# Two additions moved from VectorE into TensorE's accumulations, with ScalarE copying the sums out of PSUM, in a Mamba block with two gated feed-forwards

## The chip, the cores and the metric

The kernel runs on one core of a Trainium2 chip. The time is the device time of one execution in microseconds (us). The core's engines are TensorE (PE in the profile; PEld is its loading of weights), VectorE (DVE), ScalarE (ACT), GpSimd (POOL) and SyncE (SP), which here only issues transfers (DMA). Each engine works through its own list of instructions in order and waits for the others by semaphores; a transfer is issued by an engine's queue and carried out by the core's 16 DMA engines.

## The reference, cut to what matters

The input x has 4 sequences of 1024 tokens and 256 features, all in float32.

```python
u  = rmsnorm(layernorm(x)) * norm1_w
z, xb, B, C, dt = split(u @ in_proj.T)             # per token
dt = softplus(dt @ dt_proj.T + bias)               # 256 channels
h_t = exp(dt_t * A) * h_{t-1} + (dt_t * xb_t) * B_t   # 32 states a channel
y  = sum_states(h * C) + D_param * xb              # "D x"
hr = layernorm(x) + (y * silu(z)) @ out_proj.T
hr = hr + (silu(xn @ gate.T) * (xn @ up.T)) @ down.T      # xn = rmsnorm(hr)
x1 = x + hr
out = x1 + fwht(silu(n @ W1.T) * (n @ W3.T)) @ W2.T       # n = layernorm(x1)
```

The change touches two of these sums: `D_param * xb` in y, and the residual rows `hr` (with x already added to them in the kernel) behind the down projection.

## The kernel before, in words

Work goes by chunks of 512 tokens: 8 chunks, numbered 0 to 7, two to a sequence. Even chunks are first halves of a sequence and their scans start from zero; odd chunks are second halves, whose scans start from states that POOL kept (L783). Each chunk has 16 steps, n = 0 to 15, and a step is a sixteenth of the 8192 channel-state rows: four blocks of 128 partitions by 512 tokens. For a step q

- SP issues a transfer of dt, spread over the partitions, into `da` (L704 through `dma_da`, 1 MB, four buffers), and two of dt times xb into `ub` (512 KB each, six buffers);
- ACT takes the exponential of `da` in place (L741, four of 128x512), running one step ahead of the scans;
- DVE multiplies `ub` by B, which lies in PSUM as `pb`, into `bx` (L765, two of 128x1024), and scans `da` in place (L774, four of 128x512);
- POOL multiplies the states by C, with `cr` from a transfer (L784, one of 128x2048);
- PE sums over the states into `py` in PSUM (L795, four products into four 32-partition strips, which run side by side). Steps 0 to 7 go to one `py`, steps 8 to 15 to the next; `py` has one buffer.

A `da` buffer is free again when PE has summed its step, so the transfer for step q + 4 is issued after the sums of step q.

`y_dx` (L810, DVE) then makes yt = x * D + py in one operation, and `y_z` (L815, POOL) multiplies it by silu(z). Both happen twice a chunk, once behind n = 7 and once behind n = 15.

`pb` is written once for eight steps by `copy_b` (L754): at n = 0 of a chunk by ACT, at n = 8 by DVE.

All else of the block (norms, projections, two gated feed-forwards) is laid between the steps. The order is written by hand: a tick is half a step, `at(tick, lane, function)` puts a function on a tick, and the loop at the end of `tile_block` runs each tick's lanes in the order PE, ACT, `times_b`, ACTb, two exponentials (of the next step), a scan, DVE, a scan, POOL0, `times_c`, POOL, `sum_states`, PEend, ACTend, SP, `dma_ub`, `dma_da`, `dma_cr`, SPend. There are 32 ticks to a chunk. E is the first tick behind a chunk's own steps, which is the first tick of the next chunk, and what `post` does for a chunk it does at E + something, beside the next chunk's steps:

- E+2 (ACTend): ACT's copies of a later chunk's transposed input and of the rest of the second feed-forward before it. E+3: `hr` = layernorm(x) (ACT, L200); out projection on PE from yt and `wo` (`add_rows`, L306); its sums are copied by ACT (`evict`, L321) and added by POOL (`add_pool`, L325) for chunks 0 to 6.
- E+4 to E+7: on PE the down projection of the second feed-forward of the chunk before (`w2h`, L306).
- E+5 to E+9: row sums by ACT (`row_stats`, L170 and L173), the root on POOL (L195, L196), scaled rows on ACT (L200), transposes on PE (L213); x is added to `hr` by POOL (L659).
- E+10 to E+16: first gated feed-forward: projections on PE (L226, `gated`), silu (L263) and copies (L270) on ACT, products on POOL (L274).
- E+18 to E+21: down projection by `add_rows` with `wd`, one 128-token group a tick (L306). Its sums of two groups at a time are added to `hr` by DVE in `add` (L316), at E+20 and E+22.
- E+20 to E+25: row sums of `hr` by ACT behind that (ACTend of E+20 and E+22), the root on POOL, scaled rows on ACT, transposes on PE.
- E+26 to E+39: second gated feed-forward (L226 from `xt`) and its down projection; the store at E+43.

For chunk 7 all of this comes behind the last scan, as a tail. There the sums of the out projection and of the last down projection are added by DVE (`add`).

Of the kernel before, what the change touches and what calls it, by code (L numbers as in the profile page):

```python
# [9 lines left out]
F32 = mybir.dt.float32  # L10
AF = mybir.ActivationFunctionType
ALU = mybir.AluOpType
# [3 lines left out]
P = 128  # L16
# [4 lines left out]
TT = T // P  # L21
# [6 lines left out]
def tile_block(ctx: ExitStack, tc: tile.TileContext, a, out):  # L28
# [20 lines left out]
    nc = tc.nc  # L49

    wp = ctx.enter_context(tc.tile_pool(name="w", bufs=1))
    p1 = ctx.enter_context(tc.tile_pool(name="p1", bufs=1))
# [4 lines left out]
    sm = ctx.enter_context(tc.tile_pool(name="sm", bufs=4))  # L57
# [23 lines left out]
    us = [{"b": b, "c": c} for b in range(BATCH) for c in range(SEQ // T)]  # L81
    load_x(us[0])
    n1 = load("n1", [P, 2], a["n1"])
    ident = load("ident", [P, P], a["ident"])
# [8 lines left out]
    dpar = load("dpar", [P, 2], a["dpar"])  # L93
    rsel = load("rsel", [P, 8, 32], a["rsel"])

    mhalf = wp.tile([P, TT], F32, tag="mhalf", name="mhalf")
    nc.vector.memset(mhalf, -0.5)
    w2h = wp.tile([P, 8, DM], F32, tag="w2h", name="w2h")
# [83 lines left out]
    def row_stats_first(u, src):  # L182

        u["mv"] = sm.tile([P, 2, TT], F32, tag="mv", name="mv")
        st = sm.tile([P, TT, 6], F32, tag="st", name="st")
        ag = sm.tile([P, TT, 2], F32, tag="ag", name="ag")
        for t in range(TT):
            nc.vector.bn_stats(st[:, t, :], src[:, t, :])
        for t in range(TT):
            nc.vector.bn_aggr(ag[:, t, :], st[:, t, :])  # L190
        nc.vector.tensor_copy(u["mv"][:, 1, :], ag[:, :, 1])
        nc.vector.tensor_scalar(u["mv"][:, 0, :], ag[:, :, 0], -1.0 / 16, None, ALU.mult)
# [45 lines left out]
    def at(tick, lane, fn, *args):  # L238
        todo[tick][lane].append(partial(fn, *args))
# [53 lines left out]
        for i in range(1, len(chunks)):  # L293
            at(tick + 3, "POOL", product, i)

    def add_rows(tick, u, lhs, rhs, per_tick, lane="PE", on_pool=False):

        po = {}

        def pe(t):  # L300
            if t % 2 == 0:
                po[t // 2] = dense_psum().rearrange("p (t d) -> p t d", t=2)
            left, right = lhs(), rhs()
            n = len(left)
            for k in range(n):
                nc.tensor.matmul(  # L306
                    po[t // 2][:, t % 2, :],
                    lhsT=left[k][:, t * P : (t + 1) * P],
                    rhs=right[k],
                    start=(k == 0),  # L310
                    stop=(k == n - 1),
                )

        def add(i):
            hr = u["hr"][:, 2 * i : 2 * i + 2, :]
            nc.vector.tensor_tensor(hr, hr, po[i], ALU.add)  # L316

        def evict(i):
            ev = p3.tile([P, T], F32, tag="up", name="ev")
            po[i] = ev.rearrange("p (t d) -> p t d", t=2), po[i]  # L320
            nc.scalar.copy(*po[i])  # L321

        def add_pool(i):
            hr = u["hr"][:, 2 * i : 2 * i + 2, :]
            nc.gpsimd.tensor_tensor(hr, hr, po[i][0], ALU.add)  # L325

        for t in range(TT):
            at(tick + t // per_tick, lane, pe, t)
            if t % 2:
                after = tick + t // per_tick + 1  # L330
                if on_pool:
                    at(after, "ACTend", evict, t // 2)
                    at(after + 1, "POOL", add_pool, t // 2)
                else:
                    at(after, "DVE", add, t // 2)
# [268 lines left out]
    def post(u, E, other):  # L604
# [31 lines left out]
        def store():  # L636
# [11 lines left out]
            lambda: [W["wo"][:, k, :] for k in range(2)],  # L648
            4,
            "PEend",  # L650
            on_pool=u is not us[-1],
        )
        at(E + 5, "ACTend", lambda: row_stats(u, u["hr"], (0, 1), False))
        at(E + 6, "ACTend", lambda: row_stats(u, u["hr"], (2, 3), False))
# [8 lines left out]
        for i in range(2):  # L663
# [5 lines left out]
            lambda: [u["m"][:n, c, :] for c, n in enumerate(sizes)],  # L669
            lambda: [W["wd"][:n, c, :] for c, n in enumerate(sizes)],  # L670
            1,
        )
        at(E + 20, "ACTend", lambda: row_stats(u, u["hr"], (0, 1)))
        at(E + 22, "ACTend", lambda: row_stats(u, u["hr"], (2, 3)))
# [6 lines left out]
        for i in range(3):  # L681
# [4 lines left out]
            lambda: [u["g"][:, c, :] for c in range(8)],  # L686
            lambda: [w2h[:, c, :] for c in range(8)],
            1,
            on_pool=u is not us[-1],
        )  # L690
        at(E + 43, "SPend", store)

# [95 lines left out]
    def sum_states(q):  # L788
        s = qs[q]
        u = s["u"]  # L790
        first, last = s["n"] % 8 == 0, s["n"] % 8 == 7
        if first:
            u["py"] = ps_y.tile([P, T], F32, tag="y", name="py")
        for b in range(4):
            nc.tensor.matmul(  # L795
                u["py"][32 * b : 32 * b + 32, :],
                lhsT=rsel[:, 2 * s["j"] + s["g"], :],
                rhs=s["da"][:, b, :],
                start=first,
                stop=last,  # L800
            )
        if last:
            at(2 * q + 4, "DVE", y_dx, u, s["h"])
            at(2 * q + 5, "POOL0", y_z, u, s["h"])


    def y_dx(u, h):
        if h == 0:
            u["yt"] = p3.tile([P, 2, T], F32, tag="T", name="yt")
        nc.vector.scalar_tensor_tensor(  # L810
            u["yt"][:, h, :], u["xr"][:, h, :], dpar[:, h : h + 1], u["py"], ALU.mult, ALU.add
        )

    def y_z(u, h):
        nc.gpsimd.tensor_tensor(u["yt"][:, h, :], u["yt"][:, h, :], u["zs"][:, h, :], ALU.mult)  # L815


    for k, u in enumerate(us):
# [8 lines left out]
    at(-20, "PE", wake_pe)  # L827
    at(-18, "ACTend", load_first)
    at(-17, "ACTend", weights_ready)
    at(-2, "DVE", times_b, 0, 0)  # L830
    at(-2, "SP", dma_da, 1)
    at(-1, "SPend", dma_cr, 0)
# [129 lines left out]
```

## Time and profile before

| what | us |
|---|---|
| median of three runs (lowest, highest) | 1163.14 (1161.78, 1168.64) |
| the profiled execution | 1173.07 |
| its span, from the first instruction to the last | 1171.2 |
| scans, from the first of chunk 0 to the end of the last of chunk 7 | 22.07 to 1053.61 |
| chunks 1 to 7 begin with their first scan at | 160.10, 286.51, 416.64, 544.81, 672.90, 801.46, 926.98 |
| busy: PE, DVE, ACT, POOL | 959.6, 962.9, 782.2, 887.1 |
| `y_dx` L810, 16 of 128x512 | 11.7 busy, 733 ns each |
| `add` L316, 20 of 128x512 (14 of them before 1050 us, six in the tail) | 13.4 busy, 669 ns each |
| `copy_b` L754 on ACT, 7; on DVE, 8 | 592 ns, 674 ns each |
| ACT's copies out of PSUM of 128x512, L270 | 579 ns each |
| granted clock of TensorE, mean | 0.899 |

How to read it: "busy" is the time in which an engine had an instruction under way; a row `out<-in` of the profile names the tile written and those read; in a list of waits the numbers are the idle time in total, how often, and the longest; a row of the timeline has its start, its length, the engine, the line, the operation and how many instructions were merged, and in brackets how long the engine had been idle before it and what ended that. PE's records of one float32 product are two. Matmul records overlap, since PE is pipelined, so the length of a merged row divided by its count says more than the mean length of one record.

### The profile page before, as it was taken

The page shows a single profiled execution, that of the slowest core. Times are in us where ns is not written, and L with a number is a line of the kernel's source. Part 1 is how long each engine was busy: PE and PEld are TensorE (multiplying, and loading weights), DVE is VectorE, ACT ScalarE, POOL GpSimd, SP SyncE. Part 2 cuts the span into 40 slices and gives each one's busy share as a digit, 9 for nine tenths or more (in the row PEclk, how much of TensorE's full clock was granted, in tenths as well). Part 3 has the DMA queues.
Part 4 walks back from the last instruction along what each step waited for, and adds up shares of the span by engine and source line. Part 5 has one row for each costly group of instructions (what it writes and reads, how often), then busy time and mean ns, then how long its engine had stood idle before and what let it go on. Part 6 is the DMA issues. An engine that isn't in the chain of part 4 may idle for free.

```text
span 1171.2 us, 11883 instructions
## 1 busy us (share of the span) xinstructions
PE 959.6 (82%) x3374; PEld 456.5 (39%) x3374; DVE 962.9 (82%) x840; ACT 782.2 (67%) x1411; POOL 887.1 (76%) x515
## 2 busy tenths in 40 slices
PE   8464236969998799969996999979997987799978
PEld 3121012423634255423633364424543362336535
DVE  4897799999998989999999899999999899990000
ACT  3835556868768786779677786878685967563331
POOL 6675758878978888878977998789977898674312
PEclk9777558979899799979998899979997999789989
DMA  7989999898799889997799889988799789730000
GB/s 252 352 300 351 353 327 308 311 325 296 250 340 320 300 298 320 319 327 281 270 348 325 281 300 334 319 325 297 270 310 360 281 291 343 262 111 1 18 0 18
DMA packets 89441, 321.89 MB, mean 275 GB/s; under 512 B 9312, under 2 KB 20000, under 8 KB 73120
## 3 DMA queue, kind: packets, MB, share of 16 engines
q1 hardware_dynamic: 87520, 318.38, 77.1%
q10 hardware_dynamic: 1856, 2.75, 0.7%
q8 instruction: 27, 0.44, 0.1%
q14 instruction: 38, 0.31, 0.1%
HBM read 302.22 MB, written 18.87 MB: 274 GB/s over the span
## 4 chain that ended last, share of the span: by engine, by line
PE 25%; DMA 7%; DVE 6%; POOL 6%; issue 5%; ACT 4%; DVEq 0%; POOLq 0%; ACTq 0%; SPq 0%
PE dense L226 14%; PE dense L306 8%; DMA da<-dtd 5%; POOL da L784 4%; DVE da L774 3%; DVE bx L765 3%; PE py L795 3%; DMA ub<-ud 2%; ACT da L741 1%; POOL m L274 1%; POOL g L274 1%; DVE hr L316 0%; ACT up L270 0%; ACT L741 0%; ACT junk L173 0%
## 5 line engine op out<-in xcount | busy, mean ns | idle before, releaser
L784 POOL TENSOR_TENSOR da<-da,cr 128x2048 f32<-128x2048 f32 x128 | 580.0, 4531 | 86.8 <-DVE da L774 22.5
L741 ACT ACTIVATE da<-da,nega 128x512 f32<-128x512 f32 x508 | 334.4, 713 | 170.8 <-DMA da<-dtd 159.3
L774 DVE TENSOR_TENSOR_SCAN da<-da,carry,bx 128x512 f32<-128x512 f32 x256 | 315.7, 1268 | 20.0 <-DVE bx L765 7.6
L774 DVE TENSOR_TENSOR_SCAN da<-da,bx 128x512 f32<-128x512 f32 x256 | 300.2, 1209 | 37.0 <-ACT da L741 21.3
L765 DVE TENSOR_TENSOR bx<-ub,pb 128x1024 f32<-128x1024 f32 x254 | 312.2, 1229 | 20.3 <-ACT pb L754 9.3
L795 PE MATMUL py<-da,rsel 128*32 128x512 f32 x1024 | 162.5, 712 | 159.4 <-POOL da L784 159.4
L226 PE MATMUL dense<-xt,w 128*128 128x512 f32 x512 | 238.4, 621 | 1.4 <-ACT si L263 1.4
L226 PEld LDWEIGHTS dense<-xt,w 128*128 128x128 f32 x512 | 99.4, 199 | 145.9 <-issue 123.4
L795 PEld LDWEIGHTS py<-da,rsel 128*32 128x32 f32 x1024 | 21.4, 115 | 243.0 <-POOL da L784 201.2
L306 PE MATMUL dense<-w2h,g 128*128 128x256 f32 x512 | 113.4, 380 | 0.0
L274 POOL TENSOR_TENSOR g<-si,up 128x512 f32<-128x512 f32 x64 | 80.5, 1272 | 32.3 <-ACT up L270 32.2
L306 PEld LDWEIGHTS dense<-w2h,g 128*128 128x128 f32 x512 | 96.8, 190 | 18.4 <-ACT ev L321 2.5
L306 PE MATMUL dense<-wd,m 128*128 128x256 f32 (+1 forms) x384 | 98.2, 400 | 0.9 <-POOL m L274 0.9
L316 DVE TENSOR_TENSOR hr<-hr,dense 128x512 f32<-128x512 f32 x20 | 13.4, 669 | 99.9 <-PE dense L306 99.9
L226 PE MATMUL dense<-ut,win 128*128 128x512 f32 x192 | 94.7, 625 | 0.2 <-ACT ut L220 0.2
L270 ACT COPY up<-dense 128x512 f32<-128x512 f32 x112 | 63.4, 579 | 46.8 <-PE dense L226 46.4
L274 POOL TENSOR_TENSOR m<-si,up 128x512 f32<-128x512 f32 (+1 forms) x48 | 60.2, 1270 | 43.5 <-ACT up L270 43.5
L226 PE MATMUL dense<-ht,wg 128*128 128x512 f32 x192 | 87.7, 600 | 3.4 <-ACT ht L220 3.4
L306 PEld LDWEIGHTS dense<-wd,m 128*128 128x128 f32 (+1 forms) x384 | 68.6, 192 | 37.6 <-issue 20.6
L263 ACT ACTIVATE si<-dense 128x512 f32<-128x512 f32 x112 | 60.7, 596 | 28.4 <-PE dense L226 25.5
L226 PE MATMUL dense<-ht,wu 128*128 128x512 f32 x160 | 72.8, 600 | 4.8 <-ACT si L263 4.8
L741 ACT ACT_TABLE_LOAD x44 | 56.5, 1283 | 4.8 <-DMA da<-dtd 4.0
(95 smaller groups left out, 798.6 us busy)
## 6 DMA issues: line engine op xcount, KB each, us to landing
da<-dtd SPq DMA_DIRECT2D x127, 1024.0 KB
ub<-ud SPq DMA_DIRECT2D x254, 512.0 KB
cr<-cd SPq DMA_DIRECT2D x64, 256.0 KB
x<-in_x SPq DMA_DIRECT2D x8, 512.0 KB
dtd<-dt SPq DMA_DIRECT2D x16, 256.0 KB
ud<-du SPq DMA_DIRECT2D x16, 256.0 KB
cd<-cc SPq DMA_DIRECT2D x16, 256.0 KB
out<-hr SPq DMA_DIRECT2D x8, 512.0 KB
```

The lines of the kernel that those rows point to most:

```text
L226: nc.tensor.matmul(dst[:n], lhsT=w[:, k, col : col + n], rhs=src[:, k, :], start=(k == 0), stop=(k == 1),)
L263: nc.scalar.activation(g[i]["si"][:n], g[i]["pg"][:n], AF.Silu)
L270: nc.scalar.copy(g[i]["up"][:n], g[i]["pu"][:n])
L274: nc.gpsimd.tensor_tensor(u[dst][:n, c, :], g[i]["si"][:n], g[i]["up"][:n], ALU.mult)
L306: nc.tensor.matmul(po[t // 2][:, t % 2, :], lhsT=left[k][:, t * P : (t + 1) * P], rhs=right[k], start=(k == 0), stop=(k == n - 1),)
L316: nc.vector.tensor_tensor(hr, hr, po[i], ALU.add)
L741: nc.scalar.activation(da, da if q else s["u"]["pdt", b], AF.Exp, scale=an[:, s["h"], s["j"], b, s["g"] : s["g"] + 1],)
L765: nc.vector.tensor_tensor(s["bx"], s["ub", b0 // 2], u["pb"].unsqueeze(1).broadcast_to([P, 2, T]), ALU.mult)
L774: nc.vector.tensor_tensor_scan(da, da, s["bx"][:, b % 2, :], start, ALU.mult, ALU.add)
L784: nc.gpsimd.tensor_tensor(s["da"], s["da"], s["cr"].unsqueeze(1).broadcast_to([P, 4, T]), ALU.mult)
L795: nc.tensor.matmul(u["py"][32 * b : 32 * b + 32, :], lhsT=rsel[:, 2 * s["j"] + s["g"], :], rhs=s["da"][:, b, :], start=first, stop=last,)
```

## The change

D x becomes part of PE's accumulation in `py`. At the start, ACT makes two diagonal matrices of D (`dd`, one for each half of the channels) from the identity. Where a `py` begins (n = 0 and n = 8), PE first multiplies `dd` by `xr`, the rows of x, into it (start of the accumulation), and the sums over the states add to that. `y_dx` is gone. In its place ACT copies `py` to `yt` at the end of the same tick (lane ACTend), and `y_z` follows on POOL as before. For the last `py` of all there is no copy: DVE multiplies `py` by silu(z) at once.

In `add_rows` with `wd`, each 128-token group begins with a product of the identity with the residual rows `hr`, and the six products of the down projection add to it. `add` on DVE becomes a copy by ACT, `replace`, from PSUM into `hr`, at the same ticks in lane ACTend, ahead of the row sums that read it. This holds for all eight chunks. The other two uses of `add_rows` stay as they were.

Two small tiles of the very first row statistics move to a pool with one buffer; no instruction changes by that.

```diff
+    dd = wp.tile([P, 2, P], F32, tag="dd", name="dd")
+
+    def diagonal(h):
+        nc.scalar.activation(dd[:, h, :], ident, AF.Identity, scale=dpar[:, h : h + 1])
...
-        st = sm.tile([P, TT, 6], F32, tag="st", name="st")
-        ag = sm.tile([P, TT, 2], F32, tag="ag", name="ag")
+        st = p1.tile([P, TT, 6], F32, tag="st", name="st")
+        ag = p1.tile([P, TT, 2], F32, tag="ag", name="ag")
...
+            dst = po[t // 2][:, t % 2, :]
+            if way == "pe":
+                rows = u["hr"][:, t, :]
+                nc.tensor.matmul(dst, lhsT=ident, rhs=rows, start=True, stop=False)
             for k in range(n):
                 nc.tensor.matmul(
-                    po[t // 2][:, t % 2, :],
+                    dst,
                     lhsT=left[k][:, t * P : (t + 1) * P],
                     rhs=right[k],
-                    start=(k == 0),
+                    start=(k == 0 and way != "pe"),
                     stop=(k == n - 1),
                 )
...
+        def replace(i):
+            nc.scalar.copy(u["hr"][:, 2 * i : 2 * i + 2, :], po[i])
...
-                if on_pool:
+                if way == "pe":
+                    at(after, "ACTend", replace, t // 2)
+                elif way == "pool":
                     at(after, "ACTend", evict, t // 2)
                     at(after + 1, "POOL", add_pool, t // 2)
                 else:
...
         if first:
             u["py"] = ps_y.tile([P, T], F32, tag="y", name="py")
+            x = u["xr"][:, s["h"], :]
+            nc.tensor.matmul(u["py"], lhsT=dd[:, s["h"], :], rhs=x, start=True, stop=False)
         for b in range(4):
...
-                start=first,
+                start=False,
                 stop=last,
             )
         if last:
-            at(2 * q + 4, "DVE", y_dx, u, s["h"])
-            at(2 * q + 5, "POOL0", y_z, u, s["h"])
-
-
-    def y_dx(u, h):
+            if q == NQ - 1:
+                at(2 * q + 4, "DVE", y_z_last, u)
+            else:
+                at(2 * q + 4, "ACTend", y, u, s["h"])
+                at(2 * q + 5, "POOL0", y_z, u, s["h"])
+
+
+    def y(u, h):
         if h == 0:
             u["yt"] = p3.tile([P, 2, T], F32, tag="T", name="yt")
-        nc.vector.scalar_tensor_tensor(
-            u["yt"][:, h, :], u["xr"][:, h, :], dpar[:, h : h + 1], u["py"], ALU.mult, ALU.add
-        )
+        nc.scalar.copy(u["yt"][:, h, :], u["py"])
...
+    def y_z_last(u):
+        nc.vector.tensor_tensor(u["yt"][:, 1, :], u["py"], u["zs"][:, 1, :], ALU.mult)
...
+    for h in range(2):
+        at(1, "ACTend", diagonal, h)
```

More of the change, by code (lines that the diff above doesn't have):

```diff
@@ L294, in gated, with add_rows @@
             at(tick + 3, "POOL", product, i)
-    def add_rows(tick, u, lhs, rhs, per_tick, lane="PE", on_pool=False):
+    def add_rows(tick, u, lhs, rhs, per_tick, lane="PE", way=None):
         po = {}
@@ L650, in post @@
             "PEend",
-            on_pool=u is not us[-1],
+            way="pool" if u is not us[-1] else None,
         )
@@ L671, in post @@
             1,
+            way="pe",
         )
@@ L688, in post @@
             1,
-            on_pool=u is not us[-1],
+            way="pool" if u is not us[-1] else None,
         )
```

## The prediction

> **What bounds the kernel now.** I read the page's busy shares first, then the busy time by stage, the waits of VectorE (DVE), and the timeline where a chunk begins and where its second half runs. Chunks, steps (n = 0 to 15), ticks and E are those of the section on the kernel.
>
> ```profile
> PE 959.6 (82%) x3374; PEld 456.5 (39%) x3374; DVE 962.9 (82%) x840; ACT 782.2 (67%) x1411; POOL 887.1 (76%) x515
> ```
> Two engines share the first place. Chunks 4 and 5 by themselves:
>
> ```profile
> core 0: us, PE busy (x) PEld busy (x) DVE busy (x) ACT busy (x) POOL busy (x), PEclk, DMA share, GB/s
> ...
> 545.00:671.00 126.00, 112.20 (x403) 54.21 (x402) 115.75 (x100) 94.55 (x175) 107.80 (x67) 0.92 0.85 305
> 671.00:801.00 130.00, 118.40 (x432) 56.00 (x430) 121.95 (x102) 101.89 (x185) 110.38 (x56) 0.95 0.89 313
> ```
> DVE works 92 to 94% of such a stretch, PE 89 to 91%, DMA 85 to 89%. Three resources stand within 6% of each other, so DVE's share alone doesn't settle what an edit on it is worth. Its waits do more:
>
> ```profile
> DVE hr L316 <- PE dense L306: 99.9, 6, 43.9
> DVE da L774 <- ACT da L741: 21.5, 18, 4.2
> DVE yt L810 <- PE py L795: 12.5, 7, 8.9
> ...
> DVE bx L765 <- ACT pb L754: 9.3, 3, 4.1
> ```
> The 99.9 us are the tail behind the scans, where DVE has nothing else to do. The last line is the one that matters: at the start of chunks 3, 5 and 7 DVE stands still (3.16, 4.09 and 2.04 us in the timeline) for ScalarE's (ACT's) copy L754. How ACT comes to be late there, in chunk 4:
>
> ```profile
> 616.64 0.51 SPq L704 DMA_DIRECT2D da<-dtd  x1
> ...
> 621.90 1.06 PE L795 MATMUL py<-da,rsel 128*32 128x512 f32 x8 [0.18 <-POOL da L784]
> ...
> 622.90 6.03 PE L306 MATMUL dense<-wd,m 128*128 128x256 f32 x24
> ...
> 629.83 1.33 ACT L741 ACTIVATE da<-da,nega 128x512 f32<-128x512 f32 x2 [4.82 <-POOL carry L783]
> ...
> 640.31 0.19 POOL L195 TENSOR_SCALAR s<-mv 128x4 f32<-128x4 f32 x1 [5.24 <-ACT junk L173]
> ...
> 642.54 4.53 POOL L784 TENSOR_TENSOR da<-da,cr 128x2048 f32<-128x2048 f32 x1
> ...
> 647.13 1.93 PE L795 MATMUL py<-da,rsel 128*32 128x512 f32 x8 [1.43 <-POOL da L784]
> ...
> 666.56 7.13 PE L226 MATMUL dense<-xt,w 128*128 128x512 f32 x16
> ...
> 670.84 0.60 ACT L754 COPY pb<-br 128x512 f32<-128x512 f32 x1
> 671.46 1.23 DVE L765 TENSOR_TENSOR bx<-ub,pb 128x1024 f32<-128x1024 f32 x1 [4.09 <-ACT pb L754]
> ```
> Read it as a relay: a transfer issued at 616.64 lets ACT go on at 629.83 (the carry copy named there is 0.19 us long; in chunk 5 the same wait names the transfer). ACT is then busy without a gap until 640.24, POOL waits 5.24 us for its row sums, PE runs from 647.13 to 670 without a gap, and ACT's copy comes last. No instruction of DVE lies on this chain: it runs beside DVE, and at the end of a first half it is the longer of the two.
>
> **The change, part by part.** The sum is made against the profiled execution's own 1173.07 us; the median shown is 9.93 us less, and I carry that distance over.
>
> *DVE loses work.* Two scans back to back take 2.45 us in a second half. With `add` (L316) between them they run from 753.58 to 756.62, 0.59 more; with `y_dx` (L810) from 745.30 to 748.40, 0.65 more; where it waits for PE, from 680.66 to 684.83, 1.72 more. Fourteen additions lie before the tail: 8.3. Of fifteen `y_dx` before the last, three wait 0.95 (5.2 with it), three 0.24 (3.0), nine not (5.9). Together 22.4 us of DVE. [...] The trace shows DVE idle at three chunk starts with this work still on it, so I book less.
>
> *What DVE's gain is worth.* From the start of chunk 3 to that of chunk 5 (and 5 to 7) the end is set by the relay. DVE being earlier moves the relay only where the relay waits for DVE: into chunks 2, 4 and 6 PE waits 2.40, 2.03 and 2.36 us for POOL's product, which follows the scans. That is all that can be gained per pair. Chunk 7 is different: from n = 1 on the exponentials end 5 to 10 us ahead of their scans, so DVE sets the pace until the last scans, and its 1.72 + 0.65 + 2 x 0.59 = 3.5 come off. In chunk 0 ACT waits for transfers at nearly each step (0.93 of DMA from 60 to 190 us): its one `y_dx` buys nothing.
>
> *ACT gains four copies a chunk.* L270 copies 128x512 out of PSUM in 579 ns. Two of the four (`replace`) fall between 629.83 and 640.24, before the row sums: 1.16 us on the relay for each of chunks 1 to 6; if ACT's wait for the transfer shrank as much, zero. The two `y` copies lie beside ACT's waits (4.82 before 629.83); without these they would cost 0.58 each. [...]
>
> *PE gains products.* The trace has no `dd` product. Its nearest row is 16 records of the same 128x512 shape in 7.13 us; each fp32 product is two records (L226 has 512 from xt for the code's 256), so 0.89 (1.07 at the slow 8.59 after an idle gap). Sixteen make 14.3. The residual rows are 128x256: 32 L306 records took 7.07, so 0.44 each, 32 make 14.1. Where they lie decides:
> - At a chunk's start, tick E+3, `dd` waits for `y`, which now stands behind ACT's other work of tick E+2:
>
> ```profile
> 682.90 0.75 DVE L810 SCALAR_TENSOR_TENSOR yt<-xr,dpar,py 128x512 f32<-128x512 f32 x1 [0.95 <-PE py L795]
> ...
> 684.05 1.07 PE L795 MATMUL py<-da,rsel 128*32 128x512 f32 x8 [0.27 <-POOL da L784]
> ...
> 685.20 1.26 POOL L815 TENSOR_TENSOR yt<-yt,zs 128x512 f32<-128x512 f32 x1
> ...
> 686.31 1.11 ACT L200 ACTIVATE hr<-x,s 128x256 f32<-128x256 f32 x2
> ...
> 686.52 3.29 PE L306 MATMUL dense<-wo,yt 128*128 128x256 f32 x14 [0.78 <-POOL yt L815]
> ```
>   `y` takes the place of hr at 686.31 and ends at 686.87; `dd` ends at 687.8, the sums at 688.8, and the products that began at 686.52 begin at 689.25: PE is 2.75 us later. Behind it wait 64 records of `w2h` and the next da transfer; POOL's `y_z` moves 1.7 and holds POOL's queue. The same reckoning gives 2.8 into chunk 3, 0.7, 1.1, 1.05, 1.2 into 1, 2, 4, 6 and 0.3 into 7.
> - At n = 8 and 9 PE now finishes 0.17 to 0.18 us before POOL does (621.90). `dd` and two residual products put the sums 1.78 later at n = 8, 2.67 at n = 9, and with them the next da transfers. I take zero on the path: the da transfer of 616.64 was used 13.2 us later, one of 658.75 only 5.2 us later, so 8 us of it was queue, and a later issue waits less. Without that cover it is 2.67 a chunk.
>
> *Small edits.* Two diagonals on ACT: between L824's 259 ns and 601 ns of L200, so 0.5 to 1.2 us at tick 1, beside transfers. The statistics tiles' pool is no instruction. No transfer is added; SP's da issues move with the sums above. `y_z_last` does in one 0.69 us DVE operation what `y_dx` and `y_z` did from 1062.52 to 1064.66: 1.3 less in the tail. There the residual products cost 3 x 0.44 = 1.3 (the first fills a wait for POOL), ACT's copy saves 0.1: the tail nets -0.1.
>
> *Sum.* Chunks 1 and 2: 0.7 + 1.16 - 2.40 + 1.1 + 1.16 = +1.7. Chunks 3 and 4: 2.8 + 1.16 - 2.03 + 1.05 + 1.16 = +4.1. Chunks 5 and 6: 2.75 + 1.16 - 2.36 + 1.2 + 1.16 = +3.9. Chunk 7: -3.5. Tail: -0.1. Total +6.1: 1179.2 for a profiled execution, 1169 for the median. The lower end, where buffers swallow every shift: 3 x -2.27 - 3.5 - 0.1 = -10.4, 1153. The upper end adds, at five boundaries, the 1.7 by which `y_z` holds POOL's queue: 1178.
>
> **The rivals.**
> *DVE sets the pace after all.* For it: it works without a gap longer than 1 us from 672.9 to 921, and every da is ready before its scan in second halves. Against: the three stops at chunk starts. If the relay also runs faster once scans are early, all 22.4 come off: 1141. It decides if the relay waits for DVE at more than one place a pair.
> *The ties at n = 8 and 9 are not covered.* SP issues in order, so a late da also holds the ub transfers behind it. Seven chunks by 2.67 make 18.7 on top: 1188, slower than before. It decides once the queue in front of a da is shorter than 2.7 us; the 8 us above speak against.
> *The copies starve the exponentials.* Four by 0.58 in seven chunks, 16.2, on top: 1185. ACT's 170.8 us idle before L741 speak against it.
>
> **How the numbers follow.** The forecast's case 0.54, DVE's 0.22, the ties 0.16, the copies 0.08. The likeliest gives 1169, by itself 1153 to 1178. Both signs hold much, so the range reaches into DVE's case and into the ties': 1146 to 1185. One per cent (11.6 us, about what a measurement tells from no change) puts the borders at 1151.5 and 1174.8: faster 0.24 (DVE's case and a sliver of the forecast's), same 0.46, slower 0.30 (the ties, the copies, the forecast's upper end).
>
> **What would show it.** Right: DVE's wait for pb L754 grows from 9.3 us to about 15 or more, its busy time falls by some 23, its waits for ACT's da grow; PE waits for `y` ahead of the `dd` product into chunks 3 and 5; POOL's wait for row sums grows by 1 a chunk. Wrong: pb waits no longer than before and the scans end near 1031 instead of 1053.6 (DVE's case), or da transfers landing later by the delay of their issue at n = 12 (the ties).

## The result, and the profile after

| | median of the runs, us | lowest to highest | profiled execution (span) |
|---|---|---|---|
| before | 1165.52 (4 runs) | 1161.78 to 1168.64 | 1173.07 (1171.2) |
| after | 1179.08 (4 runs) | 1176.34 to 1183.37 | 1183.37 (1181.6) |

The ratio is 1.0123, with a 95% interval of 1.0084 to 1.0162: the change makes the kernel 1.2% slower, 13.6 us. The profiled executions lie 7.6 us (before) and 4.3 us (after) above their medians, so a difference of a microsecond or two between single chunks of the two traces proves nothing; medians decide on amounts, and the traces show places. Ratios and intervals leave out executions that lie over 1.5% above the fastest of their kernel; this matters for one experiment only (e6, `dd` left out), where it takes three of ten, while its median is that of all ten.

The busy times, from the page of the kernel after:

```profile
PE 991.4 (84%) x3470; PEld 474.7 (40%) x3470; DVE 942.6 (80%) x809; ACT 800.0 (68%) x1444; POOL 885.9 (75%) x514
```

DVE has 20.3 us less to do, PE 31.8 us more, ACT 17.8 us more. PE's growth is more than the 28.4 us of its new products (14.3 + 14.1 in the prediction): some of the new ones run at a lowered clock, as the rows below show. The waits after:

```profile
ACT da L758 <- DMA da<-dtd: 152.7, 53, 9.9
...
DVE da L791 <- ACT da L758: 49.2, 42, 3.4
...
POOL s L201 <- ACT junk L179: 41.7, 6, 14.0
...
PEld py L812 <- ACT yt L832: 38.0, 8, 14.2
PE py L812 <- ACT yt L832: 34.8, 8, 13.3
...
DVE bx L782 <- ACT pb L771: 17.5, 5, 4.5
```

L758, L771, L782 and L791 are the lines before's L741, L754, L765 and L774; L812 is the `dd` product, L832 the copy of `py`. DVE's wait for `pb` has grown from 9.3 us to 17.5 and from three chunk starts to five, its wait for ACT's exponentials from 21.5 to 49.2. There is a wait that was not there at all: PE stands 34.8 us for ACT's copy of `py`, eight times. The longest of these, 13.3 us, is in chunk 0; in the kernels below that keep the copy on ACT a wait of 9.6 to 14.4 us stands there too, early copy or late. The other seven are the starts of chunks 1 to 7. Here is that of chunk 5 (its first scan is at 679.54):

```profile
691.53 1.05 ACT L226 COPY ut<-dense 128x512 f32<-128x512 f32 x2
692.48 0.60 ACT L276 COPY up<-dense 128x512 f32<-128x512 f32 x1
692.95 0.61 ACT L832 COPY yt<-py 128x512 f32<-128x512 f32 x1
...
693.61 2.08 PE L812 MATMUL py<-xr,dd 128*128 128x512 f32 x2 [3.19 <-ACT yt L832]
...
695.62 1.58 PE L814 MATMUL py<-da,rsel 128*32 128x512 f32 x8
...
697.12 3.72 PE L317 MATMUL dense<-wo,yt 128*128 128x256 f32 x16
697.38 0.51 SPq L721 DMA_DIRECT2D da<-dtd  x1
```

The reader sees ACT's copy stand behind the copies of the same tick, PE idle for 3.19 us until it is done, the product then take 2.08 us, and behind it the sums, the out projection and, since it waits for the sums, the next da transfer. The product itself is no 2.08 us piece of work: at n = 8 of the chunks, where PE does not wait for the copy, its two records take 1.12 to 1.13 us. What makes it long is PE's clock, 0.57 in the mean from 693.60 to 697.20. The same place in chunk 4, first the timeline and then the stretches (the column after POOL busy is the granted clock, 1.00 being full speed):

```profile
560.94 2.08 PE L812 MATMUL py<-xr,dd 128*128 128x512 f32 x2 [3.65 <-ACT yt L832]
...
562.94 1.93 PE L814 MATMUL py<-da,rsel 128*32 128x512 f32 x8
...
564.80 4.79 PE L317 MATMUL dense<-wo,yt 128*128 128x256 f32 x16
```

```profile
core 0: us, PE busy (x) PEld busy (x) DVE busy (x) ACT busy (x) POOL busy (x), PEclk, DMA share, GB/s
540.00:557.20 17.20, 17.08 (x56) 6.71 (x54) 13.47 (x12) 16.88 (x26) 16.34 (x7) 1.00 0.83 281
557.20:560.90 3.70, 0.08 (x1) 0.00 (x0) 3.56 (x4) 3.70 (x9) 1.98 (x2) 0.90 0.78 312
560.90:565.00 4.10, 4.06 (x11) 0.90 (x12) 3.83 (x4) 4.10 (x8) 3.96 (x4) 0.50 0.92 290
565.00:569.60 4.60, 4.60 (x17) 3.91 (x18) 4.23 (x5) 0.88 (x2) 4.60 (x3) 0.78 0.66 254
```

After 3.7 us without a product the clock is 0.50 for the next 4.1 us and in the mean 0.78 over 4.6 more; taken between the moments at which it changes, it is 0.50 from 560.17 to 567.00 and 1.00 on both sides. The product, the sums (1.93 us instead of 1.06) and the out projection (4.79 instead of 3.72) all pay: 2.9 us on top of the wait.

How late PE is at each start can be read from one number, the end of the out projection counted from the chunk's first scan:

| into chunk | 1 | 2 | 3 | 4 | 5 | 6 | 7 | sum |
|---|---|---|---|---|---|---|---|---|
| before | 17.10 | 18.73 | 16.92 | 17.47 | 16.91 | 17.27 | 16.91 | |
| after | 17.69 | 19.85 | 22.83 | 22.73 | 21.31 | 22.65 | 17.29 | |
| later by | 0.6 | 1.1 | 5.9 | 5.3 | 4.4 | 5.4 | 0.4 | 23.1 |
| predicted | 0.7 | 1.1 | 2.8 | 1.05 | 2.75 | 1.2 | 0.3 | 9.9 |

And the chunks' lengths, from first scan to first scan (the last to the end of the scans), with the tail behind:

| chunk | 0 | 1 | 2 | 3 | 4 | 5 | 6 | 7 | tail |
|---|---|---|---|---|---|---|---|---|---|
| before | 138.0 | 126.4 | 130.1 | 128.2 | 128.1 | 128.6 | 125.5 | 126.6 | 117.6 |
| after | 134.5 | 124.2 | 131.9 | 133.3 | 132.7 | 130.3 | 130.7 | 123.2 | 117.8 |

The loss lies in chunks 2 to 6, where PE starts late. Chunks 1 and 7, where it is on time, are shorter than before, as one would wish of a change that takes work from DVE.

### The profile page after: what moved, and what is told of

Same layout as the page of the kernel before. It is cut to its first block, busy times and chain, and to the rows that moved or that the text cites. A ratio compares the mean times of both kernels' runs of the same rounds, so it can differ in the third digit from the quotient of the medians.

```text
span 1181.6 us, 12107 instructions
## 1 busy us (share of the span) xinstructions
PE 991.4 (84%) x3470; PEld 474.7 (40%) x3470; DVE 942.6 (80%) x809; ACT 800.0 (68%) x1444; POOL 885.9 (75%) x514
## 3 DMA queue, kind: packets, MB, share of 16 engines
q10 hardware_dynamic: 1856, 2.75, 0.6%
## 4 chain that ended last, share of the span: by engine, by line
PE 47%; ACT 13%; DMA 10%; POOL 8%; issue 5%; DVE 3%; SPq 0%; DVEq 0%; POOLq 0%; ACTq 0%
PE dense L232 24%; PE dense L317 15%; DMA da<-dtd 7%; PE py L814 6%; POOL da L801 6%; ACT da L758 5%; DMA ub<-ud 3%; DVE da L791 2%; DVE bx L782 1%; ACT L758 1%; ACT junk L179 1%; PE py L812 1%; ACT junk L176 1%; ACT up L276 1%; POOL m L280 1%
## 5 line engine op out<-in xcount | busy, mean ns | idle before, releaser
L758 ACT ACTIVATE da<-da,nega 128x512 f32<-128x512 f32 x508 | 335.5, 713 | 166.0 <-DMA da<-dtd 152.7
L791 DVE TENSOR_TENSOR_SCAN da<-da,bx 128x512 f32<-128x512 f32 x256 | 298.9, 1208 | 52.1 <-ACT da L758 37.6
L791 DVE TENSOR_TENSOR_SCAN da<-da,carry,bx 128x512 f32<-128x512 f32 x256 | 314.1, 1267 | 28.9 <-ACT da L758 11.6
L782 DVE TENSOR_TENSOR bx<-ub,pb 128x1024 f32<-128x1024 f32 x254 | 312.2, 1229 | 28.1 <-ACT pb L771 17.5
L814 PE MATMUL py<-da,rsel 128*32 128x512 f32 x1024 | 158.8, 696 | 87.3 <-POOL da L801 87.3
L280 POOL TENSOR_TENSOR g<-si,up 128x512 f32<-128x512 f32 x64 | 80.7, 1273 | 41.8 <-ACT up L276 41.7
L317 PEld LDWEIGHTS dense<-w2h,g 128*128 128x128 f32 x512 | 96.8, 190 | 18.4 <-issue 5.5
L317 PE MATMUL dense<-wd,m 128*128 128x256 f32 (+1 forms) x384 | 94.9, 388 | 0.5 <-POOL m L280 0.5
L276 ACT COPY up<-dense 128x512 f32<-128x512 f32 x112 | 63.3, 580 | 45.3 <-PE dense L232 45.1
L327 DVE TENSOR_TENSOR hr<-hr,dense 128x512 f32<-128x512 f32 x4 | 2.8, 688 | 101.3 <-PE dense L317 101.3
L219 PE MATMUL dense<-ident,hn 128*128 128x128 f32 x128 | 30.4, 361 | 40.7 <-ACT hn L206 40.3
```

Source lines behind the costliest of these rows:

```text
L219: nc.tensor.transpose(u["pt"][k][:, t * P : (t + 1) * P], src[:, t, k * P : (k + 1) * P], ident)
L276: nc.scalar.copy(g[i]["up"][:n], g[i]["pu"][:n])
L280: nc.gpsimd.tensor_tensor(u[dst][:n, c, :], g[i]["si"][:n], g[i]["up"][:n], ALU.mult)
L317: nc.tensor.matmul(dst, lhsT=left[k][:, t * P : (t + 1) * P], rhs=right[k], start=(k == 0 and way != "pe"), stop=(k == n - 1),)
L758: nc.scalar.activation(da, da if q else s["u"]["pdt", b], AF.Exp, scale=an[:, s["h"], s["j"], b, s["g"] : s["g"] + 1],)
L782: nc.vector.tensor_tensor(s["bx"], s["ub", b0 // 2], u["pb"].unsqueeze(1).broadcast_to([P, 2, T]), ALU.mult)
```

## The experiments

The theory formed from these rows: the loss is the place of ACT's copy of `py` at a chunk's start. The `dd` product may not write `py` before that copy has read it, the copy stands at the end of its tick's ACT work, and PE is idle until then and slow behind it. The rivals: the copies' time on ACT ahead of the row sums; the new products at n = 8 and 9; the `dd` product's own length; DVE as the bound. All edits are to the kernel after unless it is said otherwise, and all ratios are to the kernel before, run on the same chip (medians 1165.69, 1165.64 and 1166.61 us in the three groups e1 to e4, e5 to e8, e9 to e12).

| run | what it is | median, us | ratio (95%) |
|---|---|---|---|
| e1 | D x alone | 1176.45 | 1.0094 (1.0057 to 1.0131) |
| e2 | residual rows alone | 1161.60 | 0.9969 (0.9953 to 0.9985) |
| e3 | both, `py` copied by DVE | 1158.79 | 0.9953 (0.9933 to 0.9973) |
| e4 | both, ACT's copy early in its tick | 1156.04 | 0.9920 (0.9890 to 0.9950) |
| e5 | both, DVE multiplies `py` by silu(z), no copy | 1157.31 | 0.9933 (0.9917 to 0.9949) |
| e6 | copy late, no `dd` product | 1173.69 | 1.0034 (0.9998 to 1.0070) |
| e7 | copy early behind n = 15 only | 1155.65 | 0.9922 (0.9893 to 0.9951) |
| e8 | copies stay, no identity products | 1175.64 | 1.0078 (1.0050 to 1.0106) |
| e9 | D x alone, copy early | 1155.19 | 0.9908 (0.9879 to 0.9937) |
| e10 | as e4, `dd` product twice | 1158.98 | 0.9942 (0.9921 to 0.9964) |
| e11 | before, `pb` at n = 0 copied by DVE | 1166.96 | 1.0015 (0.9997 to 1.0033) |
| e12 | as e4, `pb` at n = 0 copied by DVE | 1155.33 | 0.9910 (0.9881 to 0.9938) |

**e1 and e2: each half by itself.** In e1 the residual rows are added by DVE again; in e2 D x is made by DVE as before, and only the residual rows go through PE.

```diff
             lambda: [W["wd"][:n, c, :] for c, n in enumerate(sizes)],
             1,
-            way="pe",
         )
```

> D x alone: the residual rows are added by VectorE as before. Three theories of the 13.6 us lost. Late copy: at a chunk's start the dd product waits 3.2 us for ScalarE's copy of py and then runs 2.1 us instead of 1.1; it expects nearly all of the loss here, +9 to +14 us against before (1174 to 1180). Ties: the added products put the sums of n = 8 and 9 later; dd is one half of the first, so it expects about +6. Row sums: the copies into hr ahead of the row sums lengthen the relay; it expects -3 to +3 here.

Measured: 1176.45 us, as the late copy expects. The wait of PE for the copy is there in full (37.7 us, nine times), that of DVE for da is 40.4.

```diff
-            x = u["xr"][:, s["h"], :]
-            nc.tensor.matmul(u["py"], lhsT=dd[:, s["h"], :], rhs=x, start=True, stop=False)
...
-                start=False,
+                start=first,
...
-            if q == NQ - 1:
-                at(2 * q + 4, "DVE", y_z_last, u)
-            else:
-                at(2 * q + 4, "ACTend", y, u, s["h"])
-                at(2 * q + 5, "POOL0", y_z, u, s["h"])
+            at(2 * q + 4, "DVE", y, u, s["h"])
+            at(2 * q + 5, "POOL0", y_z, u, s["h"])
...
-        nc.scalar.copy(u["yt"][:, h, :], u["py"])
+        nc.vector.scalar_tensor_tensor(
+            u["yt"][:, h, :], u["xr"][:, h, :], dpar[:, h : h + 1], u["py"], ALU.mult, ALU.add
+        )
...
-    for h in range(2):
-        at(1, "ACTend", diagonal, h)
```

> The residual rows alone: y_dx stays on VectorE as before, no dd product. Late copy expects -4 to +3 us against before (VectorE is rid of 14 additions, ScalarE's row sums begin 1.2 us later a chunk). Ties expects +6 to +8, row sums +8 to +13.

Measured: 1161.60 us. The residual half is a gain of 4.1 us by itself, although both `replace` copies stand ahead of ACT's row sums and identity products stand ahead of the sums at n = 8 and n = 9, two each. So neither of these is what makes the change slow; the loss is in the D x half. The halves do not add up (10.8 lost and 4.1 gained, 13.6 lost by both); the difference of 7 us is hardly more than the noise of three medians.

**e3, e4 and e5: the same sum, the copy elsewhere.** e3 lets DVE copy `py` where `y_dx` stood. e4 leaves the copy on ACT and moves it from the end of its tick's ACT work to the start: the same instructions on the same engines. e5 has no copy; DVE multiplies `py` by silu(z) at once, for every `py`, and POOL has none of these products.

```diff
-                at(2 * q + 4, "ACTend", y, u, s["h"])
+                at(2 * q + 4, "DVE", y, u, s["h"])
...
-        nc.scalar.copy(u["yt"][:, h, :], u["py"])
+        nc.vector.tensor_copy(u["yt"][:, h, :], u["py"])
```

> The changed kernel with the copy of py done by VectorE at the place of the old y_dx instead of by ScalarE at the end of the tick. Late copy expects PE's wait ahead of dd at a chunk's start to fall from 3.2 us to under 1 and most of the loss to go: -3 to +4 us against before. Ties and row sums expect +9 to +14, as the changed kernel, since products and copies into hr stay.

```diff
-                at(2 * q + 4, "ACTend", y, u, s["h"])
+                at(2 * q + 4, "ACT", y, u, s["h"])
```

> The changed kernel with ScalarE's copy of py put ahead of the tick's exponentials and other copies instead of behind them, the engine and all work the same. Late copy expects the copy some 3 us earlier at a chunk's start, PE's wait there nearly gone, and -2 to +6 us against before. If it is ScalarE's or PE's amount of work, and not the place of the copy, the time stays at +12 to +15.

```diff
-            if q == NQ - 1:
-                at(2 * q + 4, "DVE", y_z_last, u)
-            else:
-                at(2 * q + 4, "ACTend", y, u, s["h"])
-                at(2 * q + 5, "POOL0", y_z, u, s["h"])
+            at(2 * q + 4, "DVE", y_z_last, u, s["h"])
...
-    def y_z_last(u):
-        nc.vector.tensor_tensor(u["yt"][:, 1, :], u["py"], u["zs"][:, 1, :], ALU.mult)
+    def y_z_last(u, h):
+        if h == 0:
+            u["yt"] = p3.tile([P, 2, T], F32, tag="T", name="yt")
+        nc.vector.tensor_tensor(u["yt"][:, h, :], u["py"], u["zs"][:, h, :], ALU.mult)
```

> The changed kernel without any copy of py: VectorE multiplies py by silu(z) straight from PSUM at the place of the old y_dx (0.69 us, fifteen more times), so ScalarE's copy and POOL's product y_z both go. Late copy expects PE's wait ahead of dd to stay under 1 us as with VectorE's copy, the out projection to start 1.3 us earlier at each chunk's start, and 3 to 8 us less than the kernel with VectorE's copy (1151 to 1156). If the amount of work on VectorE sets the pace again, the same as that kernel (1157 to 1161).

Measured: 1158.79, 1156.04 and 1157.31 us, all faster than the kernel before. e3 and e4 fell further than the late copy foresaw (to -6.9 and -9.6 us). e5 did not reach its 1151 to 1156: its out projections end 0.2 to 1.1 us earlier than e3's at six of the seven starts, nothing came of it, and 1157 is the figure of its rival, VectorE's amount of work. For e3 and e5, which leave more work on DVE than e4, that rival stays open. e4 is the cleanest of the three: nothing but an order on one engine turns 1.2% slower into 0.8% faster, 23 us. The start of chunk 5 in e4, with its first scan at 661.18:

```profile
671.94 0.58 ACT L832 COPY yt<-py 128x512 f32<-128x512 f32 x1
...
672.57 1.12 PE L812 MATMUL py<-xr,dd 128*128 128x512 f32 x2 [0.51 <-ACT yt L832]
...
673.63 1.06 PE L814 MATMUL py<-da,rsel 128*32 128x512 f32 x8
673.65 1.06 ACT L226 COPY ut<-dense 128x512 f32<-128x512 f32 x2
...
674.62 3.72 PE L317 MATMUL dense<-wo,yt 128*128 128x256 f32 x16
674.87 0.51 SPq L721 DMA_DIRECT2D da<-dtd  x1
```

The copies L226 and L276 now stand behind the copy of `py` instead of ahead of it. PE waits 0.51 us instead of 3.19, the product takes 1.12 instead of 2.08, and the sums begin 12.45 us after the first scan instead of 16.08. In e4 the out projection ends after 17.25, 16.71, 17.16, 17.17, 17.16, 17.16 and 16.90 us into chunks 1 to 7; the kernel after is 24.8 us later over the seven, and 23.0 us longer by the medians. So a delay of PE at a chunk's start is paid almost in full. The profiled executions of e1, e6, e8 and e10 bear this out: their out projections end 22.2, 17.3, 26.5 and 2.2 us later in sum than e4's, and their spans are 21.7, 20.5, 26.8 and 1.8 us longer. The count from the first scan is fair only among kernels whose scans begin alike: in e12 below the sum is 13.1 us larger and the span 0.9.

**e7: which of the two copies.** Only the copy behind n = 15, the one at a chunk's start, is early; that behind n = 7 stays at the end of its tick.

```diff
-                at(2 * q + 4, "ACTend", y, u, s["h"])
+                at(2 * q + 4, "ACT" if s["h"] else "ACTend", y, u, s["h"])
```

> The changed kernel with the early place for the copy only behind n = 15 (the chunk's start); behind n = 7 it stays at the end of the tick. If the chunk's start is where the time was lost, nearly the whole gain of the early copy: 1154 to 1160. If the copy behind n = 7 costs as much, half of it: 1164 to 1170.

Measured: 1155.65 us, not to be told from e4. The copy in the middle of a chunk costs nothing that can be seen where it stands; the one at a chunk's start is the loss.

**e6: the wait without the product.** The `dd` products are left out, so y lacks D x; the copy stays late, and the sums at n = 0 now wait for it themselves.

```diff
-            x = u["xr"][:, s["h"], :]
-            nc.tensor.matmul(u["py"], lhsT=dd[:, s["h"], :], rhs=x, start=True, stop=False)
...
-                start=False,
+                start=first,
```

> The changed kernel without the dd products; D x is left out of y, and ScalarE's copy of py stays at the end of the tick. Wait: the sums of n = 0 then wait for the copy in dd's place, so most of the loss stays, 1171 to 1177. Product: if the two records of dd, 2.1 us at a chunk's start, are what costs, the time falls to 1160 to 1166.

Measured: 1173.69 us as the median of ten executions, but these fall in two groups, three from 1158.1 to 1165.7 and seven from 1171.4 to 1178.4. The profiled one is 1175.63. It shows both kinds of start within one execution, here chunk 3 and chunk 4 (the profile puts the gap down to "issue"; in chunk 4 the copy of `py` runs from 552.40 to 553.01 and the sums begin at 553.11):

```profile
424.08 1.07 PE L812 MATMUL py<-da,rsel 128*32 128x512 f32 x8 [3.24 <-issue]
425.08 3.72 PE L317 MATMUL dense<-wo,yt 128*128 128x256 f32 x16
```

```profile
553.11 1.94 PE L812 MATMUL py<-da,rsel 128*32 128x512 f32 x8 [3.24 <-issue]
...
554.97 5.76 PE L317 MATMUL dense<-wo,yt 128*128 128x256 f32 x16
```

```profile
core 0: us, PE busy (x) PEld busy (x) DVE busy (x) ACT busy (x) POOL busy (x), PEclk, DMA share, GB/s
420.50:424.00 3.50, 0.34 (x4) 0.11 (x1) 3.40 (x3) 3.50 (x8) 1.79 (x2) 1.00 0.79 269
424.10:429.00 4.90, 4.90 (x26) 3.62 (x27) 4.63 (x4) 4.87 (x10) 4.90 (x3) 1.00 1.01 327
...
549.90:553.10 3.20, 0.00 (x0) 0.02 (x1) 3.06 (x4) 3.20 (x7) 1.43 (x3) 0.88 0.89 312
553.10:557.00 3.90, 3.89 (x13) 1.86 (x14) 3.64 (x4) 3.90 (x8) 3.82 (x4) 0.50 1.00 301
557.00:561.00 4.00, 4.00 (x16) 3.29 (x14) 3.86 (x4) 1.19 (x3) 4.00 (x2) 0.73 1.05 383
```

Twice the same gap of 3.24 us; behind the first the clock stays at 1.00, behind the second it is 0.50 for 3.90 us and 0.73 in the mean over 4.00 more, and the out projection ends 2.9 us later (18.83 and 21.74 us after the first scan). Two things follow. The product is not needed for the loss: the late copy alone brings more than half of it, some 13 us over e4 by the ratios (1.0034 and 0.9920), 17.7 by the medians, of 23.0. And the length of a gap does not decide what it costs. The clock falls to 0.50 with gaps of 3.19 us (chunk 3 of the kernel after, 427.60 to 431.40) and 3.24 as well as 3.65 (chunk 4), and not with every one. What decides between two gaps of the same length is not shown.

So the same wait can be cheap or dear, with 2.9 us between the two outcomes. That the two groups of e6 come from this was the author's estimate; only one of the ten executions has a trace, so it is not shown.

**e8 and e10: the price of the products.** e8 leaves the identity products out (so `replace` puts the down projection without the residual rows into `hr`) and keeps all copies. e10 is e4 with each `dd` product made twice (so D x counts twice).

```diff
-            if way == "pe":
-                rows = u["hr"][:, t, :]
-                nc.tensor.matmul(dst, lhsT=ident, rhs=rows, start=True, stop=False)
...
-                    start=(k == 0 and way != "pe"),
+                    start=(k == 0),
```

> The changed kernel without the identity products; the residual rows are left out of hr, and the copies into hr stay. Ties: 0.9 us of PE less ahead of the sums of n = 8 and 1.8 of n = 9, so 8 to 14 us less than the changed kernel (1165 to 1171). Late copy and row sums: 0 to 4 less (1175 to 1179).

```diff
             nc.tensor.matmul(u["py"], lhsT=dd[:, s["h"], :], rhs=x, start=True, stop=False)
+            nc.tensor.matmul(u["py"], lhsT=dd[:, s["h"], :], rhs=x, start=False, stop=False)
```

> The kernel of e4 with every product of dd issued twice, so that D x is counted twice in y. Theory (the product is cheap unless it waits): PE has gaps ahead of the sums, so sixteen more products of 0.89 us cost 0 to 4 us: 1156 to 1160. Rival (each product at a start of py lengthens the way to the next transfer of da by its own length): 15 by 0.89 to 1.12, 13 to 17 us on top: 1169 to 1173, and VectorE's wait for da grows from 17 to about 30.

Measured: 1175.64 for e8, 3.4 us under the kernel after, and 1158.98 for e10, 2.9 us over e4. In both pairs the intervals overlap. By the medians the 32 identity products and the 16 `dd` products cost some 3 us each, a fifth of their length, and it may be nothing. The rival's 13 to 17 us for e10 are out, and DVE's wait for da there (18.4 us) is as in e4 (17.1); for e8 the intervals alone would still allow the low end of the ties' 8 to 14 us, but e2, which has all of these products, is faster than the kernel before. Work of PE that waits for nothing is cheap here.

**e9: D x alone, with the copy early.** e4 with the residual rows added by DVE, as before.

> ScalarE's copy of py stands early in its tick as in e4, the products of dd stay, and the residual rows are added by VectorE again. Theory (the place of the copy was the loss, and each half of the change is worth something once it is mended): the residual part by itself took 4.1 us off (1165.7 to 1161.6), so without it the kernel of e4 (1156.0) should stand near 1160, and below the kernel before by about 5. Rival 1 (with the copy mended only the residual part gains): 1165, the same as before. Rival 2 (only D x gains): 1156, the same as e4.

Measured: 1155.19 us, the fastest of all by median. The first of the three expectations, 1160, is wrong, and the figure of the third, 1156, came: once the copy is early, the residual half, worth 4.1 us alone, adds nothing that can be seen. That the two halves take time off the same path, which stops paying at about 1155, would explain both figures; no run shows it directly.

**e11 and e12: is the wait for `pb` what costs?** In the kernel before (e11) and in e4 (e12) DVE itself copies `pb` at n = 0, between the last two scans of the chunk before, as it does at n = 8.

```diff
-        (nc.vector.tensor_copy if h else nc.scalar.copy)(u["pb"], u["br", h])
+        nc.vector.tensor_copy(u["pb"], u["br", h])
...
-        at(2 * q - 1, "DVE" if q // 8 % 2 else "ACTb", copy_b, q)
+        at(2 * q - 1, "DVE", copy_b, q)
```

> The kernel before, with the copy of B at n = 0 made by VectorE between the last two scans of the chunk before, as it already is at n = 8. Relay theory of the prediction: ScalarE is 0.59 us a chunk start shorter, and VectorE then waits for da instead of pb; 0 to 2 us off: 1163.5 to 1165.5, with VectorE's waits for pb at zero and those for da up by 5 to 9 us. VectorE as the bound: the waits of 9.3 us go and seven copies of 0.67 come, 4.6 off: 1161.

> The kernel of e4 with the copy of B at n = 0 made by VectorE. There VectorE waits 16.1 us for pb at five chunk starts. VectorE as the bound: 16.1 less 4.7, 11 off: 1145. Relay theory: 0.59 at each of five to seven starts, 3 to 4 off: 1152 to 1153, the waits for pb turned into waits for da.

Measured: 1166.96 and 1155.33 us, neither to be told from the kernel it came from. DVE as the bound is out at these places: 4.6 and 11 us were to come off. The relay's figures did not come either: in e11 DVE's waits for da were to grow by 5 to 9 us and fell from 21.5 to 17.2. The waits of e4 and of e12:

```profile
DVE da L791 <- ACT da L758: 17.1, 23, 3.3
DVE bx L782 <- ACT pb L771: 16.1, 5, 4.9
```

```profile
DVE da L791 <- ACT da L758: 29.2, 32, 3.3
```

The wait of 16.1 us for `pb` is gone, and that for da has grown by 12.1. The wait showed where DVE meets the other chain, and it moved with the meeting place: into chunks 3 to 7 of e12 both ACT's exponentials of n = 1 and the end of the out projection come 1.2 to 3.6 us later than in e4, counted from the first scan: both shift, so it is the first scan that comes earlier. ACT is 0.59 us shorter at each start too. In e11 that brought nothing, so ACT's copy of `pb` is not what that kernel waits for in the end, as the prediction had it; in e12 a gain of 3 to 4 us can't be told from none, since the noise of the difference is some 5 us.

## Why the prediction was right or wrong

The time, 1179 us, is 10 above the forecast of 1169, within its range (1146 to 1185) and just above the 1178 that the likeliest case had as its own end. By the prediction's own border of one per cent it is slower, to which it gave 0.30. Some 2.4 of the 10 us are the kernel before, whose median stood at 1163.14 then and at 1165.52 with a fourth run; the change itself costs 13.6 us where +6.1 was forecast. That the time lies within the range is in part luck: the top of the range was set for the ties at n = 8 and 9, which did not come. The relay, a chain beside DVE on which PE's and ACT's delays count, was the right picture in the main. Its sum was made of three kinds of terms, of which the runs measure the first two together:

| kind of term | predicted | measured | from |
|---|---|---|---|
| DVE's lost work (-10.4) and `replace` ahead of the row sums, six by 1.16 (+7.0) | -3.4 | -9.6 | e4 against before |
| PE late at chunk starts | +9.6 | +23.0 | after against e4 |
| sum | +6.2 | +13.4 | (after against before: +13.6) |

(The first is 2.40 + 2.03 + 2.36 a pair, 3.5 in chunk 7 and 0.1 in the tail; the last kind is the sum of its terms into chunks 1 to 6. Rounded by pairs the prediction's sum was 6.1. The measured rows meet in e4, so that they add up to the whole by construction; what they show is the split.)

*What DVE's gain is worth: about right in amount.* 22.4 us leave DVE's path, and some 10 were credited. e4 gains 9.6 us, with whatever the copies of the second kind cost already in it, and e9, which has none of those, 11.4, each with some 3.5 us of noise. Had DVE set the pace, all 22.4 would have come off; no kernel here has a median below 1155. In chunk 7 the 3.5 us came as reckoned (126.6 to 123.2), and its parts too: e2, with the additions alone gone, has 125.1, e1 and e9, with D x alone, 124.3 and 124.0 (1.2 and 2.4 were in the sum). The tail, -0.1 predicted, is at +0.2, and in the other traces between 116.4 and 121.3 us, so that nothing finer can be read from it. Chunk 0, taken at zero, is 3.5 us shorter in the trace; e11, which has neither half of the change, is shorter there by 3.2 as well, so this is the execution and not the change.

*ACT's copies ahead of the row sums: too dear.* POOL's wait for the row sums did grow (30.1 us to 41.7; about 7 was predicted). But e2, which has all of these copies, is 4.1 us faster than the kernel before, though its additions were only 8.3 us of DVE's path, so the copies cost some 4 us at most there; and e4 and e9, with and without them, can't be told apart. The prediction named the condition for zero and did not take it; that there is slack behind POOL's wait is likely and not shown.

*PE at the chunk starts: the mis-sized term.* Into chunks 3 and 5 the place was right: the copy was put at 13.41 us after the first scan, the time of `hr` before, and it is at 692.95, 13.41 us after 679.54. What failed is the price behind it. The product was costed at 0.89 us, as a row of products in full flow, and 1.07 for a slow one; it took 2.08, the sums 1.5 to 1.9 instead of 1.06, and the out projection up to 4.89 instead of 3.72, since the clock drops with PE's wait (0.57 in the mean from 693.60 to 697.20, 0.50 from 560.17 to 567.00). Predicted were 2.8 and 2.75, measured 5.9 and 4.4. Such a price was on view in the trace of before: the sums of 647.13, shown in the prediction, took 1.93 us, at a clock that was 0.50 from 634.88 to 651.95.

Into chunks 1, 2 and 7 the lateness came out right to 0.1 us (the table above), but only into chunk 7, where the clock stayed at 1.00 (918.60 to 986.80), by the prediction's reckoning. Into chunk 2 it is luck, as the rows of before and after show:

```profile
297.47 1.94 PE L795 MATMUL py<-da,rsel 128*32 128x512 f32 x8 [2.40 <-POOL da L784]
299.34 5.90 PE L306 MATMUL dense<-wo,yt 128*128 128x256 f32 x16
```

```profile
294.32 2.08 PE L812 MATMUL py<-xr,dd 128*128 128x512 f32 x2 [3.19 <-ACT yt L832]
296.32 1.54 PE L814 MATMUL py<-da,rsel 128*32 128x512 f32 x8
297.80 3.72 PE L317 MATMUL dense<-wo,yt 128*128 128x256 f32 x16
```

The clock had been lowered at this start before the change too, with a gap of only 2.40 us (0.58 in the mean from 297.47 to 305.00), and there the out projection paid; after, the product pays and the out projection does not. Chunk 1 is alike (the out projection 4.27 before and 3.72 after, the product 2.08).

Into chunks 4 and 6 a second step failed. There 1.05 and 1.2 were reckoned, since ACT had been early at those starts of the old trace: the first exponentials of n = 1 begin 1.1 us after the first scan of chunk 4 and 0.7 after that of chunk 6, and 3.0 after those of chunks 3 and 5. In the kernel after they begin 3.0 us after all four, and all four starts look alike: 5.3 and 5.4 us. PE's delay is not what brings ACT late there, since in e4, where PE is on time, it is the same. Here is chunk 4 before (first scan at 544.81) and in e4 (534.94):

```profile
545.90 1.32 ACT L741 ACTIVATE da<-da,nega 128x512 f32<-128x512 f32 x2
```

```profile
537.97 1.32 ACT L758 ACTIVATE da<-da,nega 128x512 f32<-128x512 f32 x2
```

What e4 and the kernel after share is the work taken from DVE and the copies given to ACT; in e2, which has the additions' part of both, the same times are 2.4 and 3.0 us. Either moves the scans against ACT, and no run separates them. The reckoning took the even starts from the old trace, though the change it reckoned with moves both engines.

*The rivals.* DVE's pace (1141) is refuted by e4, which has all of DVE's lost work without the late copy and gains 9.6 us of the 22.4, and by e11 and e12. The ties at n = 8 and 9 were taken as zero, rightly: `dd` at n = 8 of chunks 1 to 7 finds no wait, e2 with the identity products is faster than before, and doubled `dd` products cost 2.9 us by the medians (e10). The starved exponentials are refuted by e4, which has every one of ACT's copies and is faster than the kernel before. What made the kernel as slow as the upper rivals foresaw is none of them but the likeliest case's own term.

*The signs.* The wait for `pb` of 15 us or more (17.5), DVE's busy time (20.3 less, some 23 foreseen), da's waits and PE's wait for `y` came as written, the last at all seven starts and not at two. The `pb` line was read for too much, though: e12 takes it away and wins nothing.

What stays open: why the kernels with the copy mended all stop between 1155 and 1159, whichever work is taken from DVE or POOL. Open too is what makes PE's clock fall with one gap of 3.24 us and not with another, and how the two groups of e6 come about in executions without a trace.

## What to carry to other kernels

When an accumulation starts in a PSUM buffer that another engine must first empty, the emptying copy belongs ahead of all that its engine could do later: here one changed lane was worth 23 us, and the products moved to PE cost about 3 us a half by the medians, if anything. Cost a new wait of PE as the wait plus the slower work behind it (3.65 us and 2.9 us in chunk 4 of the kernel after), take the durations from rows at the lowered clock, and take the cost as a range, since with a wait of the same 3.24 us the clock fell to 0.50 at one place and stayed at 1.00 at another. Before a wait is taken as the bound, ask what chain ends in it; moving the copy that DVE waited for moved only the wait.

## What the runs showed of the hardware that was not expected

The same 3.24 us without a product left PE's clock at 1.00 once and at 0.50 the next time, 129 us later in the same execution, with 2.9 us between the two outcomes. The length of a gap did not tell the outcome elsewhere either: with a shorter one, 2.40 us up to 297.47, the clock in the kernel before was 0.58 in the mean from there to 305.00. Once lowered, the clock stayed at 0.50 for longer than the gap: from 560.17 to 567.00 in chunk 4 of the kernel after, where the gap of 3.65 us ended at 560.94 and PE was busy from then on. Products that find PE running, on the other hand, were cheap here even with PE at 84 to 86% busy: some 14 us of them cost about 3 us by the medians (e8, e10).
